# Four graph layers with layer norms on one core: variances from ScalarE's accumulated squares, a bias by TensorE, layer 3's heads by transposing, attention rows loaded head by head, and sum places given in turn

## The chip, the cores and the metric

The kernel runs on one core of a Trainium2 chip. TensorE (PE) multiplies matrices and transposes, VectorE (DVE) does elementwise work and reductions, ScalarE (ACT) does functions and copies, GpSimd (POOL) does what crosses partitions and issues some transfers, and SyncE (SP) issues the other transfers. Each engine works through its own queue in order; semaphores make one engine wait for another. The metric is the device time of one execution in microseconds, the median of several runs. What stands in profile rows is from one profiled execution.

## What is computed

There are 16 graphs of 1024 nodes with 128 features, `x` of shape (16, 1024, 128), and a 0/1 adjacency of shape (16, 1024, 1024). Four layers follow each other, and after each one the sum of its input and output is normed over the features:

```python
def _layernorm(x, axis=-1, eps=1e-5):
    m = jnp.mean(x, axis=axis, keepdims=True)
    v = jnp.var(x, axis=axis, keepdims=True)
    return (x - m) / jnp.sqrt(v + eps)

x = _layernorm(x + L0(x, adj))   # one head: softmax over leaky_relu(s_i + t_j) where adj, times H = xW, relu
x = _layernorm(x + L1(x, adj))   # the same with 8 heads of 16, elu at the end
x = _layernorm(x + L2(x, adj))   # mean over neighbours times W_r + x self_w.T + self_b, a layer norm with
                                 # gamma and beta, relu
x = _layernorm(x + L3(x, adj))   # 4 heads of 32: softmax(Wh Wh.T / sqrt(32)) where adj, times Wh
```

Layer 2 has a norm of its own inside, so a graph has five layer norms: one after layer 0, one after layer 1, two in layer 2, one after layer 3.

## The kernel before

All loads, sums and products are fp32; the adjacency is kept as 8-bit floats, eight tiles of 128 x 1024 per graph (`m`). A node set is kept as 8 blocks of 128 nodes (`NB` = 8), a half being 4 blocks (`HB`). The whole program is unrolled over the 16 graphs. A second, general program stands behind it for an adjacency that is not 0/1; it does not run here.

**The planner.** The kernel does not write its instructions in order. It describes steps, each with an engine, an assumed cost in us, a due time, the buffers that it reads, writes or holds, and a function that emits its instructions (`Plan.step`, L93). `Plan.run` (L141) then takes, again and again, the step that could start first by these assumed costs (among those within 0.05 us, the one due first), gives its buffers places in their pools, and emits it. A buffer takes a place when its first step is taken and gives it back after its last one. `AHEAD` (L84) limits how far past the earliest due time of what is left a step's due time may lie. The outcome is a fixed order on each engine. At run time only the semaphores count; the assumed costs and due times have shaped the order and do nothing more.

The due times come from the loop at the end (L1025 and after): graph b starts at `b * PERIOD` with PERIOD 129, and its parts lie at fixed distances from that, so that about three graphs are in work at once: layer 0 of one graph, layer 1 of it and the one before, layers 2 and 3 of earlier ones.

**Pools.** In PSUM there are two places `wk` of two banks each, for everything that passes through; two of one bank `acc1`, for the sums of layers 0 and 1; two `acc3`, for the sums of layer 3. In SBUF: `R`, two places of four rows each, and `R0`, one of one row (rows are broadcast to all partitions); `z`, eight places of 128 x 1024 for weighted adjacency tiles of layers 0 and 1; `z3`, four for layer 3. Small statistics have two places each (`little`, L298).

**A graph's parts.**

- `before0` (L436): POOL loads the eight adjacency tiles, SP loads `x` and its transpose. TensorE multiplies by `w0c` (W and two columns for s and t, 130 in all). The maximum over the partitions comes from POOL (`over_partitions`, L374); ScalarE takes exponentials; the row of exponentials is transposed, written to DRAM, and loaded back broadcast to 128 partitions (`rows_everywhere`, L414, then `R0`, L484).
- `layer0` (L499): for each half and each tile, VectorE computes max(row, q) * adjacency into `z` (L508), and TensorE multiplies it with `hd` (L520). ScalarE applies Relu with the reciprocal of the sum (L540), VectorE adds `x` (L559). Then a norm.
- `before1` (L564): transposes, products with `w1c`, maxima and rows as before, with eight heads. Each group of four heads is one load of 2048 KB into a place `R` (L618).
- `layer1` (L646): two groups of four heads; for each tile four multiplications of 128 x 1024 on VectorE (L657), then eight matmuls on TensorE (L665). At the end of a group the sums are copied, transposed and divided (L693 to L712). `last1` (L721) applies elu and adds the input. Then a norm.
- `layer2` (L740): `turned` (L364) transposes a half, `products` (L346) multiplies by `w2c` (self weights and relation weights, 256 columns). VectorE adds the bias row to the self part (L767). The relation part is split into three bf16 parts `y2` (L755 to L781). TensorE sums them over the neighbours, 192 matmuls (L794). ScalarE scales these sums by the reciprocal degree into `agg` (L816), and VectorE adds `agg` to `total` (L825). A norm, gamma, beta, relu and the input (L843 to L857), and a second norm. ScalarE turns the adjacency into its complement for layer 3 (L834).
- `before3` (L864): for each half TensorE computes the heads twice from the transposed input: by nodes (four products, L879) and by features (one product of 512 columns, L880); ScalarE copies both out (L885, L893). A bound of the squared norms gives `low`.
- `layer3` (L921): for each half and tile, scores on TensorE (L931, L940) into both `wk` places, two Exp on ScalarE (L977), one mask on VectorE (L949), weighted sums on TensorE (L961). Division, the input added (L1016), a norm, and the result is stored (L1020).

**The norm** (`layernorm`, L379): on each block of 128 features VectorE runs `bn_stats` and `bn_aggr` (L386, L387), adds EPS (L392); POOL raises to the power -0.5 (L394); VectorE forms the shift (L399); ScalarE applies scale and shift block by block (L407).

Of the kernel before, what the change touches and what calls it, by code (L numbers as in the profile page):

```python
# [76 lines left out]
class Plan:  # L77
# [6 lines left out]
    AHEAD = 240.0  # L84

    def __init__(self):
        self.steps = []
        self.places = {}

    def pool(self, name, tiles):  # L90
        self.places[name] = [Place(t) for t in tiles]

# [34 lines left out]
    def start(self, s, now):  # L127
# [6 lines left out]
        for pool, count in wanted.items():  # L134
            free = sorted(p.free for p in self.places[pool] if p.holder is None)
            if len(free) < count:
                return None
            t = max(t, free[count - 1])
        return t

    def run(self):  # L141
        now = {}
        dues = sorted(self.steps, key=lambda s: -s.due)
# [7 lines left out]
        while left:  # L151
# [14 lines left out]
            for buf in s.bufs:  # L166
                if buf.place is None:
                    buf.place = min((p for p in self.places[buf.pool] if p.holder is None), key=lambda p: p.free)
                    buf.place.holder = buf
            s.emit()  # L170
# [19 lines left out]
def tile_binary(  # L190
# [55 lines left out]
    w0c = const.tile([P, P + 2], F32, name="w0c")  # L246
# [8 lines left out]
    for name, row in (("b", self_b), ("gamma", gamma), ("beta", beta)):  # L255
        rows[name] = const.tile([P, P], F32, name=f"b_{name}_bc")
        nc.sync.dma_start(out=rows[name], in_=row.partition_broadcast(P))

    with tc.tile_pool(name="bprep", bufs=1) as prep:
        sw = prep.tile([P, P], F32, name="b_sw")  # L260
# [11 lines left out]
        nc.vector.tensor_reduce(w0c[:, P:], t0, AX.X, ALU.add)  # L272
# [31 lines left out]
    plan.pool("acc1", acc1s)  # L304
# [3 lines left out]
    places("R", 2, [P, G1, N])  # L308
    places("R0", 1, [P, N])
    places("z", 8, [P, N])  # L310
# [35 lines left out]
    def products(xT, w, due, into):  # L346
# [4 lines left out]
        def emit():  # L351
            for k in range(HB):
                nc.tensor.matmul(  # L353
                    out.t[:, k * SLOT : k * SLOT + cols],
                    lhsT=xT.t[:, k * P : (k + 1) * P],
                    rhs=w,
                    start=True,
                    stop=True,
                )

        step("PE", 1.0, due, emit, [xT], [out], holds=[into])
# [12 lines left out]
    def over_partitions(v, op, shape, due):  # L374
        got = little(f"all{shape[1]}", shape)
        step("POOL", 1.4, due, lambda: nc.gpsimd.partition_all_reduce(got.t, v.t, P, op), [v], [got], lag=0.6)
        return got

    def layernorm(y, due):  # L379

        stats, mv = little("stats", [P, NB, 6]), little("mv", [P, NB, 2])
        rstd, shift = little("rstd", [P, NB]), little("shift", [P, NB])

        def means(half):
            for k in range(half * HB, (half + 1) * HB):
                nc.vector.bn_stats(stats.t[:, k, :], y.t[:, k, :])  # L386
                nc.vector.bn_aggr(mv.t[:, k, :], stats.t[:, k, :])  # L387

        for half in range(2):
            step("DVE", 1.04, due, lambda half=half: means(half), [(y, half)], [(stats, half), (mv, half)])  # L390
        due += 2
        step("DVE", 0.1, due, lambda: nc.vector.tensor_scalar(rstd.t, mv.t[:, :, 1], EPS, None, ALU.add), [mv], [rstd])  # L392
        step(
            "POOL", 1.7, due, lambda: nc.gpsimd.tensor_tensor(rstd.t, rstd.t, neg_half, ALU.pow), [], [rstd], lag=0.5  # L394
        )
        due += 2
        step(
            "DVE", 0.1, due,
            lambda: nc.vector.scalar_tensor_tensor(  # L399
                shift.t, in0=mv.t[:, :, 0], scalar=-1.0, in1=rstd.t, op0=ALU.mult, op1=ALU.mult  # L400
            ),
            [mv, rstd], [shift],
# [33 lines left out]
    def before0(b, due):  # L436
# [9 lines left out]
        hd = G["hd"] = Buf("hd", f"hd_{b}")  # L446
        for chunk in range(2):
# [8 lines left out]
            ps, view = products(xT, w0c, due, hd)  # L456
# [3 lines left out]
                    hd.t[:, chunk * HB : (chunk + 1) * HB, : P + 2], view()  # L460
                ),
                [ps], [hd],
            )
# [17 lines left out]
        R0 = G["R0"] = Buf("R0", f"R0_{b}")  # L481
# [1181 lines left out]
```

## Time and profile before

| what | value |
|---|---|
| median of 3 runs | 2653.84 us (2652.13 to 2659.19) |
| the profiled execution: its time, its span | 2657.68 us, 2655.9 us |
| mean granted TensorE clock | 0.962 |
| TensorE busy | 2231.1 us, 84% |
| weight loads busy | 1013.1 us, 38% |
| VectorE busy | 2302.1 us, 87% |
| ScalarE busy | 1333.8 us, 50% |
| GpSimd busy | 323.1 us, 12% |
| moved by DMA | 121.44 MB, mean 46 GB/s |

A group row reads: source line, engine, operation, output<-input by the program's names, shapes, how often; then total busy us and the mean ns of one; then the idle time of the engine just before such instructions and who ended it. A row of windows gives the stretch, its length, and for each engine the busy time and, in brackets, the instructions. A row of the timeline gives start and duration in us. fp32 matmuls that are not transposes are recorded as two rows each. Durations of neighbouring rows of VectorE and ScalarE overlap a little, so the spacing of starts is shorter than a row's mean.

### The profile page before, as it was taken

The numbers are of one execution on the slowest core, as the hardware profiler recorded it, in microseconds if no ns is written. First come the engines' busy times: TensorE is split into PE (matmuls) and PEld (weight loads), VectorE is DVE, ScalarE is ACT, GpSimd is POOL, SyncE is SP. The second block draws the span as 40 slices with busy tenths as digits, with TensorE's granted clock in tenths as the row PEclk, the third lists the DMA queues.
The fourth block names the chain that finished last, engine by engine and source line by source line (L and its number), as shares of the span: only waits on it lengthen the run. The fifth ranks groups of instructions, "written<-read, shape, count | busy, mean of one in ns | idle before, by whom it ended". The sixth has DMA issues, their size and how long they took to land.

```text
span 2655.9 us, 39328 instructions
## 1 busy us (share of the span) xinstructions
PE 2231.1 (84%) x15841; PEld 1013.1 (38%) x15841; DVE 2302.1 (87%) x3747; ACT 1333.8 (50%) x2401; POOL 323.1 (12%) x265
## 2 busy tenths in 40 slices
PE   2566889898989998898998998898998998888665
PEld 2323434252534434252533444252533434232311
DVE  2699999999999999999999999999999999996322
ACT  1113445565555546555465546555555546455532
POOL 2000101011111102011111101111111201000000
PEclk9778999999999999999999999999999999999788
DMA  6310112112131212112131212212130210100000
GB/s 91 96 57 32 57 36 61 50 27 84 13 100 9 73 37 59 52 21 91 11 102 9 65 45 44 67 19 92 11 102 7 51 52 5 72 1 9 1 8 10
DMA packets 67680, 121.44 MB, mean 46 GB/s; under 512 B 5920, under 2 KB 57248, under 8 KB 63392
## 3 DMA queue, kind: packets, MB, share of 16 engines
q1 hardware_dynamic: 49056, 102.05, 10.7%
q0 software_dynamic: 18432, 16.79, 8.0%
q8 instruction: 126, 2.06, 0.3%
q14 instruction: 66, 0.54, 0.1%
HBM read 160.17 MB, written 8.98 MB: 64 GB/s over the span
## 4 chain that ended last, share of the span: by engine, by line
DVE 60%; PE 27%; ACT 5%; issue 4%; POOL 2%; DMA 1%; SPq 0%; POOLq 0%; DVEq 0%; ACTq 0%
DVE z L657 30%; PE wk L794 7%; DVE z L949 7%; PE acc L961 6%; DVE z L508 5%; PE acc L665 5%; DVE stats L386 4%; DVE mv L387 3%; PE wk L353 2%; ACT z L977 2%; POOL rstd L394 2%; PE wk L940 2%; PE acc L520 2%; PE wk L344 1%; ACT x L407 1%
## 5 line engine op out<-in xcount | busy, mean ns | idle before, releaser
L657 DVE SCALAR_TENSOR_TENSOR z<-R,q,m 128x1024 f32<-128x1024 f32 x1024 | 1261.4, 1277 | 30.2 <-PE acc L665 30.2
L977 ACT ACTIVATE z<-wk,low 128x1024 f32<-128x1024 f32 x512 | 543.1, 1110 | 397.5 <-PE wk L940 390.0
L961 PE MATMUL acc<-z,hh 128*64 128x512 f32 x2048 | 539.3, 639 | 137.6 <-ACT z L977 124.5
L665 PE MATMUL acc<-z,hh 128*32 128x512 f32 x4096 | 531.9, 626 | 142.2 <-DVE z L657 141.3
L949 DVE SCALAR_TENSOR_TENSOR z<-m,z 128x1024 f32<-128x1024 fp8e5 x256 | 312.1, 1219 | 111.6 <-ACT z L977 111.6
L407 ACT ACTIVATE x<-x,shift,rstd 128x128 f32<-128x128 f32 x640 | 259.8, 484 | 206.1 <-DVE shift L399 206.1
L394 POOL TENSOR_TENSOR rstd<-rstd,b_neg_half 128x8 f32<-128x8 f32 x80 | 191.1, 2389 | 1348.9 <-DVE rstd L392 1153.6
L940 PE MATMUL wk<-whT 32*128 32x512 f32 x2048 | 309.8, 640 | 9.2 <-DVE rest L760 9.0
L961 PEld LDWEIGHTS acc<-z,hh 128*64 128x64 f32 x2048 | 122.4, 140 | 463.2 <-ACT z L977 235.9
L520 PE MATMUL acc<-hd,z 128*128 128x129 f32 x2048 | 247.4, 282 | 32.7 <-DVE z L508 30.8
L665 PEld LDWEIGHTS acc<-z,hh 128*32 128x32 f32 x4096 | 101.5, 111 | 453.1 <-DVE z L657 236.1
L520 PEld LDWEIGHTS acc<-hd,z 128*128 128x128 f32 x2048 | 239.2, 196 | 56.8 <-issue 21.0
L794 PEld LDWEIGHTS <-m 128*128 128x128 fp8e5 x3072 | 180.4, 98 | 32.6 <-issue 32.4
L508 DVE SCALAR_TENSOR_TENSOR z<-R,q,m 128x512 f32<-128x512 f32 x256 | 173.5, 745 | 18.9 <-DMA R<-rows 18.9
L794 PE MATMUL wk<-y,m 128*128 128x128 bf16 (+1 forms) x3072 | 186.3, 221 | 4.0 <-ACT y L776 1.8
L386 DVE BATCH_NORM_STATS2 stats<-x 128x6 f32<-128x128 f32 x640 | 170.6, 267 | 2.8
L834 ACT ACTIVATE m<-m,neg_one 128x1024 fp8e5<-128x1024 fp8e5 x128 | 146.4, 1155 | 40.8 <-PE wk L794 40.8
L442 POOL DMA_DIRECT2D m<-in_adj_dram x128 | 75.6, 596 | 714.2 <-issue 363.2
L931 PE MATMUL wk<-m,far 128*128 128x512 fp8e5 x512 | 155.7, 386 | 0.3 <-DVE rest L760 0.3
L387 DVE BATCH_NORM_AGGREGATE mv<-stats 128x2 f32<-128x6 f32 x640 | 116.5, 182 | 22.1
L940 PEld LDWEIGHTS wk<-whT 32*128 32x128 f32 x2048 | 84.5, 182 | 131.9 <-issue 109.4
L540 ACT ACTIVATE x<-acc,rd 128x128 f32<-128x128 f32 x128 | 36.6, 369 | 151.0 <-DVE rd L550 151.0
(100 smaller groups left out, 1536.6 us busy)
## 6 DMA issues: line engine op xcount, KB each, us to landing
R<-rows SPq DMA_DIRECT2D x32, 2048.0 KB
m<-in_adj_dram POOLq DMA_DIRECT2D x128, 128.0 KB, 4.0
xT<-in_xT_dram SPq DMA_DIRECT2D x32, 256.0 KB
x<-in_x_dram SPq DMA_DIRECT2D x16, 512.0 KB
R<-rows SPq DMA_DIRECT2D x16, 512.0 KB
out_dram<-x SPq DMA_DIRECT2D x16, 512.0 KB
rows<-rT SPq DMA_DIRECT2D x16, 32.0 KB
b_a_bc<-in_L_gnn_a_dram SPq DMA_DIRECT2D x2, 128.0 KB
```

Source lines behind the costliest of these rows:

```text
L386: nc.vector.bn_stats(stats.t[:, k, :], y.t[:, k, :])
L394: "POOL", 1.7, due, lambda: nc.gpsimd.tensor_tensor(rstd.t, rstd.t, neg_half, ALU.pow), [], [rstd], lag=0.5
L407: nc.scalar.activation(y.t[:, k, :], y.t[:, k, :], AF.Identity, bias=shift.t[:, k : k + 1], scale=rstd.t[:, k : k + 1])
L508: nc.vector.scalar_tensor_tensor(z.t[:, (j % 2) * HALF : (j % 2 + 1) * HALF], in0=R0.t[:, cols], scalar=q.t[:, j : j + 1], in1=m[j].t[:, c ...
L520: nc.tensor.matmul(av[k // 2].t.rearrange("p (k c) -> p k c", k=2)[:, k % 2, : P + 1], lhsT=z.t[:, at : at + P], rhs=hd.t[:, j, : P + 1], ...
L657: nc.vector.scalar_tensor_tensor(z.t, in0=R.t[:, c, :], scalar=q.t[:, j, h : h + 1], in1=m[j].t, op0=ALU.max, op1=ALU.mult)
L665: nc.tensor.matmul(av[half].t[32 * c : 32 * c + 32, :], lhsT=hh.t[:, j, at : at + 32], rhs=zs[c].t[:, half * HALF : (half + 1) * HALF], st ...
L794: nc.tensor.matmul(ps.t[:, k * SLOT : k * SLOT + part.stop - part.start], lhsT=m[j].t[:, rows_i], rhs=y2.t[:, j, part], start=j == 0 and n ...
L940: nc.tensor.matmul(sc[h // 2].t[:, (h % 2) * HALF : (h % 2 + 1) * HALF], lhsT=whT.t[rows_h, j * P : (j + 1) * P], rhs=whT.t[rows_h, cols], ...
L949: nc.vector.scalar_tensor_tensor(z.t, in0=gaps[j].t[:, cols].unsqueeze(1).to_broadcast([P, 2, HALF]), scalar=0.0, in1=z.t, op0=ALU.is_equa ...
L961: nc.tensor.matmul(av[g].t[64 * h : 64 * h + 64, :], lhsT=hh.t[:, j, at : at + 64], rhs=z.t[:, h, :], start=j == 0, stop=j == NB - 1,)
L977: lambda g=g, sc=sc, zs=zs: nc.scalar.activation(zs[g].t.rearrange("p h n -> p (h n)"), sc[g].t, AF.Exp, bias=low.t, scale=S3),
```

## The change

- *Norms.* `bn_stats` and `bn_aggr` go. A norm takes `tot`, the sums of the blocks. VectorE turns them into `off`, the negative mean. ScalarE squares each block with `off` as bias and accumulates the squares, into a scratch tile `junk`. VectorE scales and adds EPS; POOL and the rest are as before. The sums come from `sums`, one `tensor_reduce` per half (after layer 1, in layer 2's second norm, after layer 3); from the accumulator of layer 0's Relu, with the negative mean of `x` out of one more column of `w0c`; and, in layer 2's first norm, from the accumulator of the multiply-add that replaces `agg`.
- *Layer 2.* The bias is split into three bf16 rows at the start. TensorE adds it, by a matmul of a 3 x 128 tile of ones with these rows ahead of each of the four products. ScalarE copies the self part. VectorE reads the neighbour sums from PSUM, scales and adds them to `total` in one operation.
- *Layer 3's heads.* TensorE computes them by features only; ScalarE copies them out; TensorE transposes the copy; ScalarE copies that.
- *Rows.* One pool `R` of seven places of one row serves layer 0 and layer 1; each head is a load of its own. `z` has ten places.
- *Planner.* The pool `acc1` gives its places in the order of due times. AHEAD is 192, PERIOD 134.3, and some costs and due times differ.

The diff, cut to its core:

```diff
-    AHEAD = 240.0
+    AHEAD = 192.0
...
+            if pool in self.turns and any(b.place is None and b not in s.bufs for b in self.turns[pool][:count]):
+                return None
...
-    w0c = const.tile([P, P + 2], F32, name="w0c")
+    w0c = const.tile([P, P + 3], F32, name="w0c")
...
+        left = prep.tile([1, P], F32, name="b_left")
+        nc.sync.dma_start(out=left, in_=self_b.rearrange("(o f) -> o f", o=1))
+        for n in range(3):
+            part = prep.tile([1, P], BF16, name=f"b_part{n}")
+            nc.vector.tensor_copy(part, left)
+            nc.vector.tensor_tensor(left, left, part, ALU.subtract)
+            nc.sync.dma_start(out=bias[n : n + 1, :], in_=part)
...
-    plan.pool("acc1", acc1s)
+    plan.pool("acc1", acc1s, in_turn=True)
...
-    places("R", 2, [P, G1, N])
-    places("R0", 1, [P, N])
-    places("z", 8, [P, N])
+    places("R", 7, [P, N])
+    places("z", 10, [P, N])
...
+                if row is not None:
+                    nc.tensor.matmul(
+                        out.t[:, at : at + P], lhsT=ones, rhs=row, start=k % 2 == 0, stop=False, skip_group_check=True
+                    )
...
-                nc.vector.bn_stats(stats.t[:, k, :], y.t[:, k, :])
-                nc.vector.bn_aggr(mv.t[:, k, :], stats.t[:, k, :])
...
+    def sums(y, half, tot, due):
+
+        ks = slice(half * HB, (half + 1) * HB)
+        step(
+            "DVE", 0.62, due, lambda: nc.vector.tensor_reduce(tot.t[:, ks], y.t[:, ks, :], AX.X, ALU.add),
+            [(y, half)], [(tot, half)],
+        )
...
+        def square(pair):
+            for k in (2 * pair, 2 * pair + 1):
+                nc.scalar.activation(
+                    junk.t, y.t[:, k, :], AF.Square, bias=off.t[:, k : k + 1], accum_out=squared.t[:, k : k + 1]
+                )
...
+            lambda: nc.vector.tensor_scalar(rstd.t, squared.t, 1.0 / F, EPS, ALU.mult, ALU.add), [squared], [rstd],
...
+            step(
+                "ACT", 0.12, due,
+                lambda view=view, chunk=chunk: nc.scalar.copy(
+                    mean.t[:, chunk * HB : (chunk + 1) * HB, :], view()[:, :, P + 2 :]
+                ),
+                [ps], [(mean, chunk)],
             )
...
+                            accum_out=tot.t[:, half * HB + 2 * n + k : half * HB + 2 * n + k + 1],
...
+        G["R"] = [Buf("R", f"R_{b}_{h}") for h in range(H1)]
+        for h, R in enumerate(G["R"]):
+            step(
+                "SP", 1.7, due + 60 * (h // G1) + h,
+                lambda h=h, R=R: nc.sync.dma_start(out=R.t, in_=kept.t[h, :].partition_broadcast(P)),
                 [kept], [R], lag=2.0,
             )
...
-            ps, view = products(xT, w2c, due + chunk, y2)
+            ps, view = products(xT, w2c, due + chunk, y2, 2.3, bias)
...
+                "ACT", 0.48, at, lambda ks=ks, view=view: nc.scalar.copy(total.t[:, ks, :], view()[:, :, :P]),
...
+                    nc.vector.scalar_tensor_tensor(
+                        total.t[:, at, :],
+                        in0=each[:, k, :P],
+                        scalar=rd.t[:, k, :],
+                        in1=total.t[:, at, :],
+                        op0=ALU.mult,
+                        op1=ALU.add,
+                        accum_out=tot.t[:, at : at + 1],
                     )
...
+            step(
+                "PE", 0.87, due + chunk,
+                lambda xT=xT, ps=ps: nc.tensor.matmul(ps.t[:, :HALF], lhsT=w3c, rhs=xT.t, start=True, stop=True),
+                [xT], [(ps, 0)], holds=[hh, whT],
+            )
...
+                lambda chunk=chunk, ps=ps: transposes(
+                    ps.t[:, HALF:], [whT.t[:, (chunk * HB + k) * P : (chunk * HB + k + 1) * P] for k in range(HB)]
+                ),
...
-                step("PE", 1.6, at, lambda j=j, sc=sc, f=scores: f(j, sc), [gaps[j], whT], sc)
+                step("PE", 1.6, at, lambda j=j, sc=sc, f=scores: f(j, sc), [gaps[j], whT, low], sc)
...
-    PERIOD = 129.0
+    PERIOD = 134.3
     for b in range(B):
         at = b * PERIOD
-        before0(b, at - 70)
+        before0(b, at - 50)
         layer0(b, at)
-        before1(b, at - 8)
-        layer1(b, at + 85, 131)
-        last1(b, at + 221)
-        layer2(b, at + 238)
-        before3(b, at + 275)
-        layer3(b, at + 295, 136)
+        before1(b, at - 76)
+        layer1(b, at + 87, 125)
+        last1(b, at + 231)
+        layer2(b, at + 234)
+        before3(b, at + 292)
+        layer3(b, at + 310, 131)
```

## The prediction

> **What bounds the kernel now.** I read the busy table first, then windows one graph long, then the chain and the groups, then the order of VectorE and TensorE inside one graph.
>
> ```profile
> PE 2231.1 (84%) x15841; PEld 1013.1 (38%) x15841; DVE 2302.1 (87%) x3747; ACT 1333.8 (50%) x2401; POOL 323.1 (12%) x265
> DVE 60%; PE 27%; ACT 5%; issue 4%; POOL 2%; DMA 1%; SPq 0%; POOLq 0%; DVEq 0%; ACTq 0%
> ```
>
> VectorE and TensorE are close, and the chain of work alternates between them. In that chain the 168-matmul piece of layer 2 returns once per graph, at 380.05, 531.24, 680.96 ... 2335.72 us: 13 periods of 150.4 us. The windows give the load of one such period and of three stages in it (the columns are the stretch, its length, then busy time of PE, PEld, DVE, ACT, POOL):
>
> ```profile
> 831.21:980.92 149.71, 136.35 (x992) 61.84 (x992) 143.18 (x234) 83.37 (x150) 20.27 (x16) 0.99 0.21 50
> 831.21:846.70 15.49, 15.18 (x211) 10.95 (x210) 13.52 (x37) 7.36 (x17) 0.00 (x0) 1.00 0.13 11
> 857.30:884.00 26.70, 26.12 (x190) 18.69 (x186) 24.90 (x64) 13.52 (x28) 3.72 (x4) 1.00 0.25 27
> 915.00:980.90 65.90, 58.63 (x364) 18.59 (x361) 63.65 (x87) 34.71 (x55) 5.55 (x4) 1.00 0.16 51
> ```
>
> Over a period VectorE is the bound: 143.2 of 149.7 us, and the listed waits in its timeline there come to 4.5 us. But stage by stage it differs. While layer 2 is summed (second row) and in layer 0 (third), TensorE is 98% busy; in layer 1 (fourth) VectorE is 97% busy and TensorE 89%. So only the layer 1 stretches can shrink directly; the others shrink only if TensorE's work is spread differently. Mean TensorE load over ten periods is 135.7 us, VectorE's 143.2, ScalarE's 83.3.
>
> The groups that the change touches:
>
> ```profile
> L407 ACT ACTIVATE x<-x,shift,rstd 128x128 f32<-128x128 f32 x640 | 259.8, 484 | 206.1 <-DVE shift L399 206.1
> L394 POOL TENSOR_TENSOR rstd<-rstd,b_neg_half 128x8 f32<-128x8 f32 x80 | 191.1, 2389 | 1348.9 <-DVE rstd L392 1153.6
> L386 DVE BATCH_NORM_STATS2 stats<-x 128x6 f32<-128x128 f32 x640 | 170.6, 267 | 2.8
> L387 DVE BATCH_NORM_AGGREGATE mv<-stats 128x2 f32<-128x6 f32 x640 | 116.5, 182 | 22.1
> ```
>
> The rows overlap a little; the timeline shows the real spacing, about 0.395 us for one pair on one 128x128 block (878.33 to 878.72):
>
> ```profile
> 878.33 0.26 DVE L386 BATCH_NORM_STATS2 stats<-x 128x6 f32<-128x128 f32 x1
> 878.62 0.18 DVE L387 BATCH_NORM_AGGREGATE mv<-stats 128x2 f32<-128x6 f32 x1
> 878.72 0.26 DVE L386 BATCH_NORM_STATS2 stats<-x 128x6 f32<-128x128 f32 x1
> ```
>
> **What the Trainium skill says.** "Perfetto Trace Analysis", section Identifying the Most-Contended Engine: occupancy is a fair measure for Vector and Scalar, matmul busy time is not for Tensor. I therefore also added TensorE's load from spacings of unstalled groups and got about 132 us per graph, against 135.7 busy; the two agree well enough to take 132 to 135.7 as its floor. "VectorE: DVE Perf Modes", section The TRN2 errata: small operations pay a fixed cost, and an fp32 `tensor_tensor` takes (N+151)/0.96 ns, 691 at 512; the trace has 692 for L712, so I use it for shapes not shown. Same page, The perf-mode tier table: `tensor_reduce` runs only at one element per cycle; L909 (1024 elements) took 1212 ns, which fits. Same page, Two Vector instructions with no wait between them: an accumulator output is a second instruction. No VectorE row here shows it; on ScalarE the read row (L834) is 204 ns, but starts 1.04 us after its main one and the next follows 0.09 us later.
>
> **The change, per graph, part by part.**
>
> VectorE removed: 40 pairs of statistics x 0.395 = 15.8; the bias addition L767, 2 x 0.60 (spacing; row 0.692) = 1.2; the addition L825, 2 x 0.61 = 1.2. Added: six `tensor_reduce` of 512 elements (last1, layer 2's second norm, layer 3; the other two norms get sums elsewhere), by half of L909 to the formula's 0.69: 0.62 each = 3.7; five `off` at the 0.1 spacing of L399 = 0.5; eight multiply-adds of 128 from PSUM with a sum. Those lie between 0.2 (the formula's 0.29 less overlap) and 0.5 (a full read of 0.2 added); I take 0.27 = 2.2, with 1.6 to 4.0 for the range. Net -18.2 + 6.4 = -11.8: VectorE 143.2 -> 131.4 busy. Gaps that are no listed wait were 149.7 - 143.2 - 4.5 = 2.0, so its floor is 133.4.
>
> ScalarE added: 40 squares of 128x128. L407 (two pointer operands) is spaced 0.385, L493 0.306; with 0.09 for the read, 0.40 to 0.475: 17.5. Sums by Relu 8 x 0.09 = 0.7; the copies of layer 2's own product 2 x 0.58 = 1.2; two copies of means 2 x 0.2 = 0.4. Removed: L816, 8 x 0.285 = 2.3. Net +17.5: 83.3 -> 101. It stays below the others on load.
>
> TensorE: bias rows 8 x (0.06, the spacing of L794's bf16 matmuls, to 0.12 if its weight load shows) = 0.5 to 1.0. Layer 3's L879, four products in about 0.95, become four transposes in 0.59 (the four L344 pieces): 2 x -0.36 = -0.7. Column 131 of w0c is lost in 0.98. Net 0: 135.7 stays, and TensorE becomes the higher of the two loads. Layer 3's heads now go TensorE, ScalarE, TensorE, ScalarE in turn. Behind the transposes that wait for ScalarE's copy stand layer 1's matmuls in TensorE's queue. The place in PSUM is held 0.9 + 0.6 + 0.6 + 0.6 + hops of about 0.8 = 3.5 against 3.1: nothing while both places are not wanted, under 1 us per graph if they are.
>
> Rows head by head: 9 row loads per graph instead of 3, 6 x 0.32 = 1.9 us of SP's issue time, and SP idles. Seven places serve what nine did (two of four heads, and one). In the built order, the tightest two: a place is freed by its last multiplication and used as head 7 after about 15 us of VectorE work, and another as the next graph's layer-0 row after 8.7 us. The 512 KB load took 7.1 us at 87.33, with adjacency loads beside it. So both are hidden; without that cover they cost at most some 2 to 5 us per graph. Behind them in SP's queue stand only the next graph's inputs, needed tens of us later.
>
> The norm's own latency: two reduces, `off` and eight squares (1.2 + 0.2 + 3.5 + two hops of about 0.3) replace eight pairs (3.2): about +2.3 us each, hidden mid-run behind layer 1's multiplications, exposed once at the start and once at the end. Three small bias transfers at the start: 3 x 0.43 on SP while it waits for VectorE's preparation anyway (xT leaves at 10.94): up to 1.
>
> Turns, AHEAD and due times move steps. I counted VectorE's multiplications between the degree steps of successive graphs. Full graphs keep 64 of layer 1, 16 of layer 0, 16 of layer 3. Before the first degree step 91 layer-1 ones stand instead of 86. After the last, 24 masks of layer 3 stand instead of 22. At the 6.7 us that a step takes in the tail (13.4 per two), +13.4. On POOL the first graph's reductions move ahead of eight adjacency loads; layer 1's start hangs on the row load (issued 95.3, used 105.5), so I count no gain.
>
> **The sum.** From the chain: 234.4 head + 145.6 + 13 x 150.4 + 131.1 + 189.1 tail = 2655.9. After: head 236.4 (+5 multiplications of 1.2, +3 norm and start, less 16 pairs of statistics, -7); first and last periods, lighter ones, 134 and 122; tail 189.1 + 13.4 + 2 = 204.5. For the period P neither engine can go under 133.4 and 135.7. VectorE today lies 4.5 us of waits above its floor; with two engines this close, each waits for the other in places, so I take 135.7 + 4 = 139.5. Then 236.4 + 134 + 13 x 139.5 + 122 + 204.5 = 2510 span; roughly 418 + 15 P. The runs' median is 2 us under the profiled span: 2508.
>
> **Rivals.** *Floor* (chance 0.20): the ten z places, 12 us of VectorE lead, smooth everything and P is 135.7 to 137.5: 2451 to 2478. For it: in layers 0 and 2 TensorE is already at 98%. *Stages do not smooth* (0.23): VectorE saves in layers 0 and 2, where TensorE sets the pace anyway. Of 40 pairs, 28 stand in the second and third window. Then P is 15.2 + 26.1 + what the rest leaves VectorE: of 104.8 there, 12 pairs (4.7) and the bias go, sums come, about 101, + 2: 144.3, 2580. Late row loads end in the same place. *ScalarE turns critical* (0.07), the one that ends slower: in its queue an Exp of layer 3 stands behind a pair of squares, 0.85 us; 20 pairs per graph, each delaying an Exp, hence the scores and masks behind it, make 17. Now that TensorE has no slack, P = 135.7 + 17 = 152.7: 2706. It decides once such delays exceed 13.5 us per graph. Against it: ScalarE idles a third of the time, and VectorE's waits for Exp are 111.6 us in all. *The saving does not show* (0.03): 2646 to 2662.
>
> **Chances and range.** Mine, P 137.5 to 142, has 0.45; 0.02 lies between the stages' case and no change. Under 0.3% this kernel's measurement tells nothing. Faster 0.90, same 0.03, slower 0.07. From 2450, where the floor ends, to 2610, inside the stages' case (P 146), leaves out under 0.2.
>
> **What would show it.** Right: VectorE's total near 2110 us, ScalarE's near 1610, TensorE's about 2230; the layer-2 pieces 139 us apart; TensorE 95% or more in full periods, with multiplications now waiting for layer 1's matmuls to free z. Wrong: waits of multiplications for row loads; matmuls of layer 3 waiting long for Exp; a period still at 144 or more with VectorE at 97% in layer 1; a tail over 215 us.

## The result, and the profile after

The change made the kernel slower. It takes 2717.78 us (median of 4 runs, 2711.09 to 2720.45), against 2653.81 for the kernel before on the same chip; the ratio is 1.023, with a 95% interval of 1.021 to 1.026. The profiled execution took 2711.09 us for a span of 2709.1, and the mean granted TensorE clock was 0.947.

The busy table and the chain of work of the changed kernel (by engine, then by line):

```profile
PE 2281.3 (84%) x15841; PEld 1011.5 (37%) x15841; DVE 2148.1 (79%) x2843; ACT 1610.2 (59%) x3745; POOL 291.8 (11%) x265
...
PE 35%; DVE 33%; ACT 26%; issue 3%; DMA 1%; POOL 1%; SPq 0%; ACTq 0%; POOLq 0%; DVEq 0%
DVE z L717 19%; ACT z L1041 11%; PE acc L1025 11%; ACT junk L438 9%; PE wk L1004 6%; PE acc L583 5%; PE wk L385 4%; PE acc L725 4%; DVE z L1013 3%; PE wk L995 3%; ACT x L461 2%; ACT m L890 2%; DVE tot L416 2%; PE wk L371 2%; DVE x L873 1%
```

The loads came out almost as forecast: VectorE 2148 us (forecast 2110), ScalarE 1610 (1610), TensorE 2281 (2230). But ScalarE, 5% of the chain before, is 26% of it now: above all Exp of layer 3 (L1041, L977 before; 11%) and the squares (L438; 9%).

From here on a period is the distance between the first degree steps (L869, L811 before) of successive graphs, as the mean of the 13 inner distances, the head is what lies before the first such step, and the tail what lies after the last. One period, in the columns of the windows shown before:

```profile
995.36:1148.72 153.36, 139.16 (x994) 61.77 (x992) 133.64 (x178) 100.09 (x234) 18.18 (x16) 0.98 0.21 49
```

VectorE is down from 143.2 to 133.6 us, and still the period is longer than before. Both large engines now idle, TensorE for 14 us and VectorE for 20 us of this period. Split at those steps, the two profiled executions are:

| part | before | after | forecast |
|---|---|---|---|
| head | 238.8 | 240.4 | about 2 more |
| first period | 145.6 | 138.5 | 134 |
| 13 periods | 150.46 each | 153.85 each | 139.5 each |
| last period | 130.7 | 129.1 | 122 |
| tail | 184.8 | 201.2 | 15.4 more |

The changes of head and tail are right within about 1 us. The miss is in the periods: 13 x 14.35 = 187 us, and 11.6 in the two lighter ones.

The groups of the changed kernel that run Exp and the squares, and those that wait:

```profile
L1041 ACT ACTIVATE z<-wk,low 128x1024 f32<-128x1024 f32 x512 | 541.0, 1106 | 322.4 <-PE wk L1004 321.9
L1025 PE MATMUL acc<-z,hh 128*64 128x512 f32 x2048 | 560.5, 660 | 190.6 <-ACT z L1041 185.6
L725 PE MATMUL acc<-z,hh 128*32 128x512 f32 x4096 | 520.3, 622 | 83.2 <-DVE z L717 83.1
L1013 DVE SCALAR_TENSOR_TENSOR z<-m,z 128x1024 f32<-128x1024 fp8e5 x256 | 312.5, 1221 | 179.5 <-ACT z L1041 179.3
L438 ACT ACTIVATE junk<-x,off 128x128 f32<-128x128 f32 x640 | 256.7, 401 | 150.1 <-DVE off L432 129.5
```

The same three groups of waiting instructions in the kernel before:

```profile
L961 PE MATMUL acc<-z,hh 128*64 128x512 f32 x2048 | 539.3, 639 | 137.6 <-ACT z L977 124.5
L665 PE MATMUL acc<-z,hh 128*32 128x512 f32 x4096 | 531.9, 626 | 142.2 <-DVE z L657 141.3
L949 DVE SCALAR_TENSOR_TENSOR z<-m,z 128x1024 f32<-128x1024 fp8e5 x256 | 312.1, 1219 | 111.6 <-ACT z L977 111.6
```

TensorE's waits for VectorE's layer 1 tiles (L725) shrank from 141.3 to 83.1 us. Its waits for Exp (L1025, L961 before) grew from 124.5 to 185.6, VectorE's (L1013, L949 before) from 111.6 to 179.3. Those are the "matmuls of layer 3 waiting long for Exp" that the prediction named as a sign against it. The timeline of the changed kernel shows how such a wait comes about:

```profile
1024.72 0.40 ACT L438 ACTIVATE junk<-x,off 128x128 f32<-128x128 f32 x1 [1.55 <-DVE off L432]
1024.81 1.99 PE L1004 MATMUL wk<-whT 32*128 32x512 f32 x8
...
1025.03 0.19 ACT L438 ACTIVATION_READ_ACCUMULATOR junk<-x,off 128x1 f32 x1
1025.25 0.40 ACT L438 ACTIVATE junk<-x,off 128x128 f32<-128x128 f32 x1
...
1028.41 0.40 ACT L438 ACTIVATE junk<-x,off 128x128 f32<-128x128 f32 x1
1028.72 0.19 ACT L438 ACTIVATION_READ_ACCUMULATOR junk<-x,off 128x1 f32 x1
1028.81 2.10 ACT L1041 ACTIVATE z<-wk,low 128x1024 f32<-128x1024 f32 x2
...
1030.96 2.40 PE L1025 MATMUL acc<-z,hh 128*64 128x512 f32 x8 [3.08 <-ACT z L1041]
```

The scores are done at about 1026.8. Both `wk` places are full of them. ScalarE is in the middle of the eight squares of a norm, 0.525 us each from start to start, and reaches Exp at 1028.81, 2.0 us after the scores. TensorE does one more piece of layer 0, up to 1027.88; its next instruction in the fixed order needs the result of Exp, and it stands still for 3.08 us. About 2.1 us of these are the two Exp themselves. Until the first Exp is done, nothing that needs a place `wk` could have stood there instead.

That layer 3's Exp holds up other work through the places shows directly in the product of a later graph's `x` with `w0c`, which has no data from layer 3. In the changed kernel it waits 37.4 us in all for Exp; in the kernel before (second row) no such wait is listed:

```profile
L385 PE MATMUL wk<-w0c,xT 128*128 128x131 f32 x256 | 44.6, 330 | 44.2 <-ACT z L1041 37.4 <-DMA xT<-in_xT_dram 6.8
L353 PE MATMUL wk<-w0c,xT 128*128 128x130 f32 x256 | 36.4, 290 | 6.9 <-DMA xT<-in_xT_dram 5.4
```

### The profile page after: what moved, and what is told of

The parts are those of the page before. It is cut to its first block, busy times and chain, and to the rows that moved or that the text cites. A ratio compares the mean times of both kernels' runs of the same rounds, so it can differ in the third digit from the quotient of the medians.

```text
span 2709.1 us, 39907 instructions
## 1 busy us (share of the span) xinstructions
PE 2281.3 (84%) x15841; PEld 1011.5 (37%) x15841; DVE 2148.1 (79%) x2843; ACT 1610.2 (59%) x3745; POOL 291.8 (11%) x265
## 4 chain that ended last, share of the span: by engine, by line
PE 35%; DVE 33%; ACT 26%; issue 3%; DMA 1%; POOL 1%; SPq 0%; ACTq 0%; POOLq 0%; DVEq 0%
DVE z L717 19%; ACT z L1041 11%; PE acc L1025 11%; ACT junk L438 9%; PE wk L1004 6%; PE acc L583 5%; PE wk L385 4%; PE acc L725 4%; DVE z L1013 3%; PE wk L995 3%; ACT x L461 2%; ACT m L890 2%; DVE tot L416 2%; PE wk L371 2%; DVE x L873 1%
## 5 line engine op out<-in xcount | busy, mean ns | idle before, releaser
L1041 ACT ACTIVATE z<-wk,low 128x1024 f32<-128x1024 f32 x512 | 541.0, 1106 | 322.4 <-PE wk L1004 321.9
L1025 PE MATMUL acc<-z,hh 128*64 128x512 f32 x2048 | 560.5, 660 | 190.6 <-ACT z L1041 185.6
L725 PE MATMUL acc<-z,hh 128*32 128x512 f32 x4096 | 520.3, 622 | 83.2 <-DVE z L717 83.1
L1013 DVE SCALAR_TENSOR_TENSOR z<-m,z 128x1024 f32<-128x1024 fp8e5 x256 | 312.5, 1221 | 179.5 <-ACT z L1041 179.3
L438 ACT ACTIVATE junk<-x,off 128x128 f32<-128x128 f32 x640 | 256.7, 401 | 150.1 <-DVE off L432 129.5
L1025 PEld LDWEIGHTS acc<-z,hh 128*64 128x64 f32 x2048 | 124.8, 144 | 502.3 <-ACT z L1041 311.7
L452 POOL TENSOR_TENSOR rstd<-rstd,b_neg_half 128x8 f32<-128x8 f32 x80 | 182.4, 2280 | 975.6 <-DVE rstd L449 960.6
L461 ACT ACTIVATE x<-x,shift,rstd 128x128 f32<-128x128 f32 x640 | 260.7, 488 | 28.8 <-DVE shift L456 28.8
L583 PE MATMUL acc<-hd,z 128*128 128x129 f32 x2048 | 255.6, 282 | 21.7 <-DVE z L571 12.2
L725 PEld LDWEIGHTS acc<-z,hh 128*32 128x32 f32 x4096 | 105.4, 111 | 387.4 <-issue 214.6
L438 ACT ACTIVATION_READ_ACCUMULATOR junk<-x,off 128x1 f32 x640 | 120.2, 188 | 0.0
L603 ACT ACTIVATE x<-acc,rd 128x128 f32<-128x128 f32 x128 | 45.2, 365 | 125.0 <-DVE rd L614 125.0
```

Of the source, the lines that this page charges most:

```text
L438: nc.scalar.activation(junk.t, y.t[:, k, :], AF.Square, bias=off.t[:, k : k + 1], accum_out=squared.t[:, k : k + 1])
L461: nc.scalar.activation(y.t[:, k, :], y.t[:, k, :], AF.Identity, bias=shift.t[:, k : k + 1], scale=rstd.t[:, k : k + 1])
L583: nc.tensor.matmul(av[k // 2].t.rearrange("p (k c) -> p k c", k=2)[:, k % 2, : P + 1], lhsT=z.t[:, at : at + P], rhs=hd.t[:, j, : P + 1], ...
L725: nc.tensor.matmul(av[half].t[32 * c : 32 * c + 32, :], lhsT=hh.t[:, j, at : at + 32], rhs=zs[c].t[:, half * HALF : (half + 1) * HALF], st ...
L1013: nc.vector.scalar_tensor_tensor(z.t, in0=gaps[j].t[:, cols].unsqueeze(1).to_broadcast([P, 2, HALF]), scalar=0.0, in1=z.t, op0=ALU.is_equa ...
L1025: nc.tensor.matmul(av[g].t[64 * h : 64 * h + 64, :], lhsT=hh.t[:, j, at : at + 64], rhs=z.t[:, h, :], start=j == 0, stop=j == NB - 1,)
```

## The experiments

Three theories. **A**: squares in ScalarE's in-order queue stand in front of Exp and of the norm's own chain, so their time lies on the path. **B**: the new order (turns, AHEAD, due times) is at fault. **C**: the work moved to TensorE (bias, heads) holds work places too long. Ratios are to the kernel before, with 95% intervals.

| run | us | ratio | period |
|---|---|---|---|
| changed kernel | 2717.8 | 1.021 to 1.026 | 153.85 |
| e1: with the old norm | 2715.0 | 1.018 to 1.022 | 154.3 |
| e2: before, with the new norm alone | 3020.2 | 1.132 to 1.138 | 177.6 |
| e3: squares costed at 1.05 a pair | 2646.7 | 0.993 to 0.997 | 148.5 |
| e4: with the old turns, AHEAD, due times | 3052.2 | 1.144 to 1.151 | 179.8 |
| e5: half of the squares | 2610.1 | 0.979 to 0.985 | 146.6 |
| e6: half as many squares again | 2872.6 | 1.079 to 1.083 | 164.0 |
| e7: with a third work place | 2499.6 | 0.938 to 0.943 | 143.0 |
| e8: before, with a third work place | 2621.4 | 0.984 to 0.988 | 153.2 |
| e9: with the old bias | 2639.6 | 0.989 to 0.994 | 148.7 |
| e10: with the old heads | 2689.5 | 1.009 to 1.013 | 152.1 |
| e11: first chosen order | 2920.5 | 1.095 to 1.099 | 169.9 |
| e12: before, order chosen likewise | 2689.0 | 1.009 to 1.012 | 153.3 |
| e13: second chosen order | 2582.9 | 0.970 to 0.975 | 145.0 |
| e14: without turns | 2742.3 | 1.030 to 1.035 | 154.0 |
| e15b: two scratch halves | 2665.5 | 1.002 to 1.006 | 150.5 |
| e16b: e13 with two scratch halves | 2581.1 | 0.970 to 0.973 | 145.1 |

**One part at a time.** e1 takes the norm (with its sums and layer 2's multiply-add) out of the change, e2 puts it alone into the kernel before, e4 takes the planner's settings back.

In e1, and the other way round in e2:

```diff
-                nc.scalar.activation(
-                    junk.t, y.t[:, k, :], AF.Square, bias=off.t[:, k : k + 1], accum_out=squared.t[:, k : k + 1]
-                )
+                nc.vector.bn_stats(stats.t[:, k, :], y.t[:, k, :])
+                nc.vector.bn_aggr(mv.t[:, k, :], stats.t[:, k, :])
...
```

In e4, with all the old offsets of the stages:

```diff
-    plan.pool("acc1", acc1s, in_turn=True)
+    plan.pool("acc1", acc1s)
-    AHEAD = 192.0
+    AHEAD = 240.0
-    PERIOD = 134.3
+    PERIOD = 129.0
...
```

> The changed kernel with the old norm (statistics by VectorE, layer 2's means by ScalarE and an addition); bias by TensorE, heads by transposing, rows head by head, turns and due times stay. Theory A, squares of 0.525 us in ScalarE's queue ahead of Exp are what made the period 153.8 us: period back to 147 to 151, time 2610 to 2665. Theory B, the new order of steps (turns, AHEAD, due times) is the cause: VectorE has 11 us more per graph and the poor order stays, 2720 to 2850. Theory C, bias and heads on TensorE: also 2700 or more.

> The kernel before with the new norm alone (sums, squares by ScalarE, layer 2's multiply-add with a sum); the bias addition, heads, rows in fours, no turns, old due times. Theory A: slower than before, period 152 to 156, 2680 to 2750, with long waits of TensorE for Exp. Theories B and C: VectorE is relieved and nothing else is harmed, period 139 to 145, 2500 to 2590.

> The changed kernel with the planner's settings of before: no turns, AHEAD 240, PERIOD 129 and the old offsets of the stages. Theory A: 2680 to 2750, period 152 to 156. Theory B: the order was the cause, period 139 to 146, 2500 to 2600. Theory C: 2680 to 2750.

No theory held in its plain form. The norm alone costs some 360 us in the old settings, more than A allowed, and TensorE's wait for Exp (L999 there) is longer than in e4 (161.2 us) and e1 (151.0). The group in e2:

```profile
L999 PE MATMUL acc<-z,hh 128*64 128x512 f32 x2048 | 594.4, 699 | 210.1 <-ACT z L1015 193.4
```

These waits are not the whole of it. For the same number of instructions (15841) TensorE is busy 138 us longer in e2 than in the kernel before (2368.7 against 2231.1), at a mean granted clock of 0.901 against 0.962; the last section comes back to this. How the rest divides is open.

The new settings save most of that loss (e4 against the changed kernel: 26 us per period), so B is wrong as put. But they do not suit the old norm (e1: 154.3, where A had 147 to 151). Order and operations belong together, and a new order alone can move the period by many us; what is left must be found without re-planning.

**The same order with fewer and more squares.** Leaving a square out of a pair, or doing one twice, changes ScalarE's load and moves no step. In e5, where a constant stands for the variances that are left out,

```diff
-            for k in (2 * pair, 2 * pair + 1):
+            for k in (2 * pair,):
...
```

and in e6

```diff
-            for k in (2 * pair, 2 * pair + 1):
+            for k in (2 * pair, 2 * pair + 1, 2 * pair + 1):
```

> The changed kernel in its own order of steps, every second square left out (one of each pair; the variances of the odd blocks are left out and a constant stands in their place). ScalarE has 10.5 us less per graph, nothing is re-planned. Theory A, the squares lie on the path that sets the period: some of it comes off the period, 4 to 7 us of 153.8 (stepping through the built order with the durations of the trace gives 4.9), 2610 to 2660. Rival, ScalarE has slack and only the order of VectorE and TensorE counts: within 1.5 us of 153.8 per period, 2695 to 2720.

> The changed kernel in its own order, one square of each pair done twice (same value, same place): ScalarE has 20 x 0.525 = 10.5 us more per graph, 111 of 154. Theory A: all of it shows, since each of the 20 pairs lies on the path: period 162 to 166, 2840 to 2910. Rival, slack of ScalarE (it idles 53 us per period): less than 3 us per period, under 2770.

10.5 us less per graph brought 7.2 per period, just over the 4 to 7 expected, and 10.5 more cost 10.2. ScalarE idles a third of the time, and yet an addition to its squares shows nearly in full. This settles A against "ScalarE has slack": the squares lie on the path. In e6 TensorE's wait for Exp grew as A has it; its group:

```profile
L1025 PE MATMUL acc<-z,hh 128*64 128x512 f32 x2048 | 575.3, 675 | 251.3 <-ACT z L1041 245.0
```

**Why a square takes 0.525 us.** Relu with an accumulator (L603) is spaced 0.34 us: its next main row starts 0.09 us after the start of the read row. After a square it is 0.22. In the built program every square waits, by a semaphore of ScalarE's own, for the square before: all write the one scratch tile. e15b gives them two halves in turn, of bf16, so the tile keeps its size; the order on each engine is that of the changed kernel.

```diff
-        junk = little("junk", [P, P])
+        junk = little("junk", [P, 2, P], BF16)
-                    junk.t, y.t[:, k, :], AF.Square, ...
+                    junk.t[:, k % 2, :], y.t[:, k, :], AF.Square, ...
...
```

> The changed kernel in its own order; the squares' scratch output alternates between two halves of a bf16 tile of the same size (the value written there is never read; the accumulated sums are as before). In the changed kernel each square waits, by a semaphore of ScalarE's own, for the square before it, since both write the one scratch tile; squares are spaced 0.525 us where Relu with an accumulator is spaced 0.34. If that wait is the excess: spacing 0.35 to 0.42, ScalarE 4 to 7 us less per graph, and as in the run with half the squares about two thirds of it come off the period: 148 to 151.5, 2635 to 2685. If the spacing is the operation's own: 0.525 stays and 2705 to 2725.

ScalarE's timeline in e15b:

```profile
706.02 0.40 ACT L438 ACTIVATE junk<-x,off 128x128 bf16<-128x128 f32 x1 [1.54 <-DVE off L432]
706.33 0.19 ACT L438 ACTIVATION_READ_ACCUMULATOR junk<-x,off 128x1 f32 x1
706.42 0.39 ACT L438 ACTIVATE junk<-x,off 128x128 bf16<-128x128 f32 x1
```

The spacing fell to 0.385 us, which is that of L461, a pass over blocks of the same size without a read: the read costs nothing any more. The period fell by 3.4 us. The kernel gains 52 us of the 64 that the change had lost; so much was a wait of an engine for itself. The new type of the scratch tile is not tried alone, but the row of a square hardly changes with it (401 ns, 392 in e15b); what shrinks is the distance from the start of the read to the next square, from 0.22 to 0.09 us. The period of 150.5 is still only that of the kernel before, though VectorE has 9.6 us less to do.

**The cost that the planner assumed.** It has 0.8 us for a pair. Two scratch halves give 0.77; the one tile gives 1.05.

```diff
-                "ACT", 0.8, due + pair, lambda pair=pair: square(pair), ...
+                "ACT", 1.05, due + pair, lambda pair=pair: square(pair), ...
```

> The changed kernel with one number changed: the planner's cost of a pair of squares 0.8 -> 1.05 us, as measured. Theory A, in the form that the plan goes wrong because it costs the squares too low: period 143 to 149, 2550 to 2640. Theory A, in the form that squares in an in-order queue delay Exp however they are placed: 150 to 155, 2670 to 2740. Theory B or C: unchanged, 2700 to 2740.

e3 takes 2646.7 us and 148.5 per period: 5.3 us per graph from one number. TensorE's wait for Exp fell to 113.4 us; the group in e3:

```profile
L1025 PE MATMUL acc<-z,hh 128*64 128x512 f32 x2048 | 548.1, 640 | 116.8 <-ACT z L1041 113.4
```

The period lies where A's first form had it, the time 7 us above. But this one number makes a new order, and that truer costs always help is not shown: e11 and e12 say otherwise.

**The work places.** e7 and e8 make a third `wk` place, by letting the two accumulators of layers 0 and 1 share a bank, and those of layer 3; the sums that share run together, so the results of these layers are lost, and only the time counts.

```diff
-    wks = [psum.tile([P, 2 * HALF], F32, name=f"wk{n}") for n in range(2)]
-    acc1s = [psum.tile([P, HALF], F32, name=f"acc1_{n}") for n in range(2)]
-    acc3s = [psum.tile([P, HALF], F32, name=f"acc3_{n}") for n in range(2)]
+    wks = [psum.tile([P, 2 * HALF], F32, name=f"wk{n}") for n in range(3)]
+    acc1s = [psum.tile([P, HALF], F32, name="acc1")] * 2
+    acc3s = [psum.tile([P, HALF], F32, name="acc3")] * 2
...
```

> The changed kernel with three PSUM work places (wk) instead of two; room is made by letting the two accumulators of layers 0 and 1 share one bank, and those of layer 3 (their sums run together, so the outputs of these layers are left wrong; the same instructions run). Costs, turns and due times as in the changed kernel, the order is planned anew. Theory A with the coupling through wk (scores need both places, each is held until its Exp, which stands behind squares): period 143 to 148, 2510 to 2600. Rival, the squares delay the norm's own chain and places do not matter: period 151 to 155, 2670 to 2730.

> The kernel before with three PSUM work places in the same way (sums of layers 0, 1 and 3 run together; same instructions). If VectorE's load (143.2 us per graph) bounds it, the third place brings 2 to 5 us per period: 145 to 149, 2550 to 2630. If the two places bind it as much as the changed kernel: period below 143, under 2530.

The changed kernel gains 218 us. The groups of e7 that waited for Exp, and below them the windows' row of one of its periods:

```profile
L1028 PE MATMUL acc<-z,hh 128*64 128x512 f32 x2048 | 540.3, 627 | 49.7 <-ACT oT L1059 27.3 <-DVE z L1016 17.6 <-ACT z L1045 4.3
...
L1016 DVE SCALAR_TENSOR_TENSOR z<-m,z 128x1024 f32<-128x1024 fp8e5 x256 | 312.6, 1221 | 45.8 <-ACT z L1045 45.7
```

```profile
957.49:1099.78 142.29, 137.06 (x994) 61.60 (x992) 132.61 (x177) 100.30 (x234) 21.33 (x17) 0.99 0.25 53
```

The wait of layer 3's sums for Exp is 4.3 us where it was 185.6, with the same squares on ScalarE. TensorE is busy for 96% of the period. So squares in front of Exp hurt through the two places: TensorE can't run on elsewhere. The order of e7 is new, though, so how much of the 10.9 us per period is the place and how much the order is not separated; that the wait for Exp all but goes is what speaks for the place. Of the 211 us between the spans, 65.6 are the tail (135.6), where little but layer 3 of the last graph is left, and 13 x 10.9 = 142 the periods.

e8 hit its total, 2621, but not as expected: its tail lost 64 us too, while its period grew to 153.2, which neither form of the expectation had. A third place is no gain by itself. TensorE's clock was low there, as the row of one of its periods shows (0.94); why this order does so is open:

```profile
994.91:1147.78 152.87, 139.19 (x994) 64.22 (x992) 142.99 (x235) 83.03 (x150) 19.39 (x16) 0.94 0.21 49
```

**The moved work (C) and the turns.**

e9 has no bias row, and the addition by VectorE (L767 of before) instead of the copy:

```diff
-            ps, view = products(xT, w2c, due + chunk, y2, 2.3, bias)
+            ps, view = products(xT, w2c, due + chunk, y2, 1.0)
-                "ACT", 0.48, at, lambda ks=ks, view=view: nc.scalar.copy(total.t[:, ks, :], view()[:, :, :P]),
...
```

e10 has both products of `before3` in one step and two copies, as before:

```diff
-                "PE", 0.87, due + chunk,
+            step("PE", 1.8, due + chunk, both, [xT], [ps])
...
```

e14 gives the `acc1` places without turns:

```diff
-    plan.pool("acc1", acc1s, in_turn=True)
+    plan.pool("acc1", acc1s)
```

> The changed kernel with layer 2's bias added by VectorE again (1.2 us per graph there, none on ScalarE and TensorE; the planner's cost of the product 2.3 -> 1.0); all else of the change kept, the order is planned anew. A product with bias takes 3.05 us by the trace against 1.0 to 1.1 without, twice per graph, in a work place. If that counts in the period: 148 to 152, 2630 to 2690. If VectorE is what counts, or the norm alone: 153 to 156, 2700 to 2750.

> The changed kernel with layer 3's heads by a second product again (both products in one step, two copies), planned anew. Stepping through the built order with measured durations gives no difference: 152 to 155 per period, 2690 to 2730. If the longer hold of the work place (product, copy, transposes, copy in turn) counts: 148 to 151, 2630 to 2680.

> The changed kernel without turns for the accumulators of layers 0 and 1 (in_turn off), AHEAD and offsets as in the change. If the turns hold work back (a rival cause): 149 to 152 per period, 2650 to 2695. If they only order what would come anyway: within 1 us of 153.8 per period, 2700 to 2735.

The bias matters: 5.2 us per period. In the timeline of the changed kernel a product with its bias row takes 0.79 us, and four of them 3.05, in a place:

```profile
1130.18 0.23 PE L382 MATMUL wk<-bias,ones 3*128 3x128 bf16 x1
1130.33 0.70 PE L385 MATMUL wk<-w2c,xTc 128*128 128x256 f32 x2
1130.96 0.23 PE L382 MATMUL wk<-bias,ones 3*128 3x128 bf16 x1
...
1133.23 0.60 PE L371 MATMUL wk<-b_ident,x 128*128 128x128 f32 x4
```

Before, four products of this shape took 1.83. That is 2.4 us more per graph on TensorE; the planner had 2.3 for the four. The heads cost 1.7 us per period; e10's period lies in the range for no difference, its total half a us below it. (e9 and e10 plan anew, so part of either gain may be the order.) The turns cost nothing per period; without them the head is 18 us longer, and e14's total lies 7 us above its expected range.

**Orders chosen by reckoning.** One can step through a built order by hand: a step starts when its engine, the steps it follows and its place are free, and takes its spacing in the trace. This gives 147.5 us per period for the kernel before and 149.5 for the changed one, 3.0 and 4.3 below what was measured. I used it to choose offsets and AHEAD. e11 also has bias and heads as before and the traces' spacings as costs:

```diff
-    AHEAD = 192.0
+    AHEAD = 214.7
-        before0(b, at - 50)
+        before0(b, at - 19.3)
-        before3(b, at + 292)
+        before3(b, at + 239.2)
...
```

e12 does the same to the kernel before. e13 has the bias as before and squares at 1.05:

```diff
-    AHEAD = 192.0
+    AHEAD = 1135.4
-    PERIOD = 134.3
+    PERIOD = 132.06
-        before0(b, at - 50)
+        before0(b, at - 44.3)
-        before1(b, at - 76)
+        before1(b, at - 330.3)
...
-        layer3(b, at + 310, 131)
+        layer3(b, at + 302.5, 131)
```

e16b is e13 with the two scratch halves of e15b.

> A version meant to be faster than both: the norm, the rows and the turns of the change; bias and heads of before; every cost that the planner is given set to the spacing in the traces (squares 1.05 a pair, product 1.08, and so on), and offsets of the stages and AHEAD chosen by trying many and stepping through each order with those durations, which gives a period of 141.5 (the changed kernel: 149.5 in the same reckoning, 153.8 measured). Expected period 143 to 147, 2540 to 2610. If such reckoning does not carry over to the chip: above 2654.

> The kernel before with only the planner's costs set to the traces' spacings (pair of statistics and so on: 1.04 -> 1.6 for four) and offsets and AHEAD chosen in the same way; no operation is changed. The reckoning gives 144.7 per period (the kernel before: 147.5 reckoned, 150.5 measured); VectorE's 143 is then nearly the whole. Expected period 146 to 149, 2580 to 2630. If the order of before was already as good as it gets: 150 or more.

> The changed kernel with two of the causes taken out (bias by VectorE as before; squares costed at 1.05 a pair) and offsets of the stages, PERIOD and AHEAD chosen again by stepping through many orders, this time also with slower GpSimd steps (a load 3.0 us, the others 1 us more) and TensorE 2% slower, which the order of the run before had not been tried against. The reckoning gives 141.1 per period, 146.2 with the slower steps. If an order with two work places can be found that cashes part of VectorE's relief: period 144 to 148, 2550 to 2620, faster than the kernel before. If the reckoning still leaves out what decides: above 2640.

> The chosen order of the run at 145.0 us per period (bias by VectorE, squares costed at 1.05 a pair, offsets chosen) with the alternating scratch output, same order. If the self-wait is the excess: squares spaced 0.35 to 0.42, period 141.5 to 144.5, 2530 to 2575. If not: 2575 to 2590.

e11 failed badly (169.9 where 141.5 was reckoned). Its groups show a large part of it: VectorE waits 236.7 us in all for the power that GpSimd takes in a norm, and in GpSimd's queue adjacency loads stand ahead of that power and wait for their places:

```profile
L450 ACT ACTIVATE x<-x,shift,rstd 128x128 f32<-128x128 f32 x640 | 255.1, 481 | 293.2 <-DVE shift L445 293.2
...
L445 DVE TENSOR_TENSOR shift<-off,rstd 128x8 f32<-128x8 f32 x80 | 13.2, 166 | 236.8 <-POOL rstd L441 236.7
```

e12 failed as well (153.3 where 144.7 was reckoned); its cause is open. In both I had set a product of 256 columns at 1.08 us where it takes 1.83, twice per graph; what that did to the orders is not shown. For e13 each order was also tried with slower GpSimd steps and a slower TensorE. It took 2582.9 us, 2.7% less than the kernel before and 5% less than the changed one. e16b does not gain on it: in this order squares spaced 0.385 us instead of 0.525 change nothing, so whether squares lie on the path depends on the order. e13, where VectorE has the bias again, also shows that two places allow 145.0 us; how much they bind depends on the order too.

## Why the prediction was wrong, point by point

- **What bounds the kernel.** "Over a period VectorE is the bound" was true of load. That TensorE and VectorE alone could keep work back was not: ScalarE, at 56% of a period before the change, had no part in the forecast period, and neither had the pair of work places.
- **Loads.** VectorE's term was good: 143.2 -> 131.4 forecast, 133.6 measured. The multiply-adds with a sum came at 0.27 us, as taken (a main row of 349 ns and a read of 84). This agrees with the Trainium skill, "VectorE: DVE Perf Modes", section Two Vector instructions with no wait between them: the read is a second instruction. ScalarE's busy total was right (100.2 us per period for 101), but what counts in a queue is the spacing, and that of the squares, 0.525 us, lay outside "0.40 to 0.475". The operation itself can do 0.385 (e15b); what the prediction left out is that each square waits for the one before.
- **TensorE "net 0"** was wrong by 4.5 us (the mean of ten periods is 140.2 against 135.7): the bias was 2.4 us where 0.5 to 1.0 was given, and the granted clock fell from 0.98 to 1.00 in such periods to 0.96 to 0.98.
- **The norm's latency, "hidden mid-run behind layer 1's multiplications"**: this failed. The 0.525 us squares are part of the path (e5, e6). What is queued behind them on ScalarE is Exp, behind Exp the two places, behind those every product and transpose.
- **The period, "135.7 + 4 = 139.5"**: the step that failed. The 4 us of waits was taken over from the kernel before, as if only TensorE and VectorE waited for each other. Measured, TensorE idles 14.2 us in the window of one period above, 11.7 of them in waits for Exp (8.7 for the sums of layer 3, 3.0 for products), and its load is higher too. With a third place (e7) the period is 143.0, still 3.5 above the forecast. That e7's time, 2499.6, lies near the forecast 2508 is luck: its tail is 65.6 us shorter, which nothing in the forecast had.
- **The planner.** The prediction looked at what turns and due times move, but not at a cost that the planner has wrong. Costs shape the order: with 1.05 for a pair the period is 148.5.
- **Rows and the tail** were right: VectorE's waits for rows are 20.9 us in all, in two waits before 100 us. Turns cost nothing per period; the heads cost 1.7 us (e10) where "under 1 us per graph" was given.
- **The rivals.** "ScalarE turns critical", given 0.07, named the mechanism (Exp behind squares), a period of 152.7 and 2706 us; it happened with 153.85 and 2718. That the figures lie so close is partly luck: it took 0.85 us for a pair that takes 1.05, a delay for each of the 20 pairs and TensorE's load as 135.7, and it did not name the work places. The evidence held against it, that ScalarE idles a third of the time, is an average; e6 shows what it was worth. It deserved more than the floor's 0.20.

## What to carry to other kernels

Before moving work to an engine with idle time, look up what stands behind it in that engine's queue, and which buffer is held until that is done: here Exp, and two PSUM places. Where an order is planned from assumed costs, a cost that is a quarter too low can lose more (5.3 us per period here) than making the operation shorter brings (3.4), so take it from a spacing in the trace; but try the new order, since e11 and e12 had costs from spacings too and were no faster. Look in the built order for waits of an engine on itself, such as a scratch output that one tile serves.

## What the runs showed of the hardware

TensorE's granted clock is halved in stretches of 3.4 us (48 of 60 in the changed kernel; the others are two or more of these on end), and in these runs such stretches follow idle gaps of TensorE. In the changed kernel after 300 us, of 91 gaps between 0.4 and 1.75 us 2 had such a stretch beginning in them or within 3.5 us after, of 36 between 1.75 and 2.75 us 20, and of 26 between 2.75 and 3.25 us 24. In the kernel before it was 3 of 149, 20 of 51 and 1 of 2. Of the 66 gaps over 1.75 us in the changed kernel, 62 are waits for Exp. Two windows of the changed kernel around the wait shown above, the gap and what follows:

```profile
1028.00:1030.90 2.90, 0.00 (x0) 0.00 (x0) 1.13 (x2) 2.87 (x6) 1.66 (x1) 1.00 0.01 3
1032.30:1035.70 3.40, 3.40 (x14) 0.65 (x10) 2.89 (x5) 2.78 (x10) 0.00 (x0) 0.50 0.48 43
```

The trace of the changed kernel has 290 us at half clock, that of before 205, that of e8 385. The Trainium skill, "TensorE: Matmul & The Clock Gate", section HAM oscillation — how this bites in real kernels, warns of idle gaps above about 3.4 us; here 2 to 3 us were often enough. So, as an estimate, a wait of 3 us costs TensorE up to 1.7 us more afterwards (half of 3.4), and I take part of the 3 to 4 us between reckoned and measured periods to be this; that is argued, not shown. It makes a wait dearer and does not explain the loss alone: e15b has 292 us at half clock, as many as the changed kernel, and is 52 us faster.
